# A two-layer graph network kernel: folded softmax sums, packed score columns and a finer hand-written order

## The chip, the cores and the metric

The kernel runs on one core of a Trainium2 chip. The metric is the device time of one execution in microseconds (us); less is better. The engines are named as in the profile: PE (matrix products; PEld is its weight load), DVE (vector), ACT (scalar and activation functions), POOL (general) and SP, which here only issues transfers (DMA).

## The reference

128 graphs of 128 nodes with 256 features pass a transformer-like layer with masked values and then a two-fold graph attention, each with a feed-forward part (FFN) and two norms.

```python
# layer 0, 8 heads of 32
scores = einsum('bhid,bhjd->bhij', q, k) / sqrt(dh)
attn = softmax(scores, axis=-1)
for r in range(4):
    out = out + einsum('bhij,bhjd->bhid', attn * (adj == r), v_r)
x = ln(src + out @ Wo + bo)
x = ln(x + gelu(x @ W1 + b1) @ W2 + b2)
# layer 1, twice: e = leaky_relu(Wh1 + Wh2^T), masked by adj > 0
att = softmax(where(adj > 0, e, NEG), axis=1)
h = att @ Wh
x = ln(x + h); x = ln(x + relu(x @ w1 + b1) @ w2 + b2)
```

adj holds only 0 and 1, so two of the four value products suffice; the kernel checks that at run time.

## The kernel before

One straight program handles 32 groups of 4 graphs (512 tokens, G = 4, P = 128, T = 512). All is float32, and each product of the program is two records in the profile. Of each group, `projected` computes q, k and v, `attention` the first layer's attention, `ffn` (called as `first_ffn` and `second_ffn`) the two feed-forward parts, `layer1` the graph attention, `norm`, `sent` and `turned` the norms and the turning of the tokens (planes of 16 bits, a transposing DMA into pT, and copies into yT). Projections and FFNs use seven block products for eight; ffn keeps one chain of them in the PSUM bank called seeded and the others in fa and fe.

The order of the work is written out by hand. FRONT, STEADY and TAIL are strings of tokens. `a:1` means: take the next step of the attention of the group one behind the base group; `*n` repeats it. Each function is a generator, and what stands between two `yield`s is one step. The names: `q` projected, `a` attention, `f` and `k` first and second FFN, `l` layer1, `n0` to `n3` norm, `t0` to `t2` turned, `bo` prepared, `in` and `rest` loads, `out` store; `gelu` and `exp` touch a function table. FRONT starts the pipeline, STEADY runs once for each of 29 base groups (a "turn"), TAIL ends it. Every engine executes its own instructions strictly in the order in which the tokens issue them; an instruction that waits holds all that come behind it on its engine, and on SP all transfers behind it. Tiles with one buffer are taken again only when their last reader has finished.

Steps that the change touches, with line numbers of the profile:

- `scores` (751, 759): products ps of q and k for a pair of graphs, 32 rows of the array each, and four Exp activations into e, a tile of 4 x 2 x 2 x 128 columns: four heads s, two graphs u of the pair, two halves c of the heads, 128 target nodes i. The 128 partitions are the source nodes.
- `masked` (769): pm = e times the adjacency, four products on DVE.
- `sums` (787, 801): pav, the value products with e and pm, and pden, the sum over all source nodes by a product with ones, four of 512 columns in 32-column tiles of the array. Then on DVE the transposes, the range checks and the reciprocal (813 to 819), and oT = pav times it (825). A pair 0 puts pden into bank fe, a pair 1 into one of the two banks s.
- `spread` (875 to 886): one score column of each of four graphs is laid along a row on all partitions, either directly (products with the identity, groups 0, 31 and in part 30) or by a transpose on PE (880), a DVE copy (882) and two transfers through DRAM (885, 886).
- `edges` (894 to 911): Identity with bias, leaky ReLU, Exp, the mask with its sums, the division.
- `prepared` (589, 593): the output bias is added to x, and a DVE instruction sums adj (adj - 1) to check it.
- `variances` (352, 354), `root` (369, 370), `affine` (381), `store` (958): the norms and the output. The variances of norm 3 stay in c_out for a check at the end.
- In `ffn` (454 to 571) a product, its evacuation and often several DVE instructions are one step.

The attention's product with ones, before:

```python
def plain():
    for s in range(HC):
        nc.tensor.matmul(
            pden[s * DH : (s + 1) * DH], k.ones, e[:, s], start=True, stop=True
        )
```

Of the kernel before, what the change touches and what calls it, by code (L numbers as in the profile page):

```python
# [31 lines left out]
class Weights:  # L32


    def __init__(self, tc, const, a):
        self.tc, self.nc, self.const, self.a = tc, tc.nc, const, a
        self.queue = tc.nc.scalar

# [3 lines left out]
    def w(self, name, t=None):  # L42
        w = self.a[name]
        if t is None:
            t = self.tile([P, w.shape[0] // P, w.shape[1]], "w_" + name)
        self.nc.sync.dma_start(t, w.rearrange("(c p) n -> p c n", p=P))
        return t

    def col(self, name, t=None):
# [3 lines left out]
        with self.nc.allow_non_contiguous_dma(reason="a bias vector as columns"):  # L53
            self.queue.dma_start(t, v.rearrange("(c p) -> p c", p=P))
        return t

    def row(self, name, first=None, t=None):
# [5 lines left out]
        if t is None:  # L63
            t = self.tile([P, n], "r_" + name)
        self.queue.dma_start(
            t, bass.AP(tensor=v.tensor, offset=v.offset, ap=[[0, P], [1, n]])
# [3 lines left out]
    def row_sum(self, n1, n2, t=None):  # L70
        r1, r2 = self.row(n1), self.row(n2, t=t)
        self.nc.gpsimd.tensor_add(r1, r1, r2)
        return r1

    def constants(self):
# [3 lines left out]
        self.ones = self.tile([P, P // 4], "ones")  # L79
        nc.vector.memset(self.ones, 1.0)  # L80
        self.eps = self.tile([P, 1], "eps")
        nc.vector.memset(self.eps, EPS)
        self.lo = self.tile([P, 1], "lo")
        nc.vector.memset(self.lo, LO)
        self.none = self.tile([1, 1], "none")
        self.mhalf = self.tile([P, G], "mhalf")
        nc.vector.memset(self.mhalf, -0.5)

# [14 lines left out]
q:0*6 a:0*3 q:0 a:0*2 b1 bo:0 a:0*2 q:1*2 a:0 q:0 q:1 gw q:1 w1 a:0 a:1 a:0 a:1 a:0*2 wqk a:1 a:0  # L103
q:1*2 n0:0 q:1 n0:0*2 a:1 n0:0 a:1*2 n0:0 a:1*3 gelu t0:0 q:1 w2 a:1 t0:0*2 f:0 a:1 in:2
output_bias f:0 a:1 f:0*2 bo:1 f:0*2 a:1 f:0 q:2 a:1 q:2 gw q:2 f:0*2 q:2 f:0 gw n0:1 f:0 q:2
f:0*2 n0:1 gw q:2 f:0*3 n0:1 f:0 n0:1 f:0*3 q:2 f:0*2 t0:1 n0:1 t0:1 n1:0 f:1 n1:0 t0:1 n1:0*2 c1
f:1*2 n1:0 q:2 f:1 q:2 t1:0 f:1 q:2 f:1 t1:0 f:1 q:2*2 u2 l:0 f:1 l:0 f:1 q:2 l:0 wv l:0*2 f:1
q:2 u1 q:2 a:2 l:0 a:2 f:1 l:0 f:1*2 l:0 f:1*2 l:0 q:2 l:0 a:2 q:2 l:0*4 q:2*2 f:1*2 q:2 l:0 exp
q:2 n2:0 q:2*4 n2:0*3 f:1 q:2 n2:0 f:1 q:2*3 t2:0 f:1 t2:0 f:1
"""  # L110
STEADY = """
f:0 a:1*2 k:-1 a:1 n1:0 t2:-1 a:1 in:2 n1:0 a:1 k:-1*2 a:1 k:-1 n1:0 k:-1*3 n1:0 a:1 n1:0 t1:0
k:-1*2 a:1 bo:1 l:0 k:-1 a:1 k:-1 a:1 t1:0 k:-1*2 a:1 k:-1 l:0 k:-1 n0:1 l:0 k:-1 n0:1*4 k:-1 q:2
k:-1 q:2 l:0 k:-1 t0:1 l:0 t0:1 q:2 k:-1*2 q:2 l:0 t0:1 f:1*4 l:0*2 q:2 k:-1 f:1 n3:-1 f:1*2 l:0
f:1 q:2*2 l:0 f:1 n3:-1*2 f:1 q:2*2 gelu f:1*3 q:2*2 out:-1 f:1 q:2 l:0 q:2 l:0 q:2*2 l:0 f:1 a:2
l:0 f:1 q:2 a:2 rest:2 q:2*2 a:2 q:2 l:0 n2:0 q:2 f:1 q:2*3 n2:0*2 f:1 q:2*2 n2:0 q:2 f:1 q:2*3
n2:0 t2:0 exp f:1 t2:0 f:1
"""
TAIL = """
f:0 a:1 n1:0 a:1 t2:-1 in:2 k:-1*2 a:1*2 k:-1 n1:0*2 k:-1 a:1*2 k:-1*2 a:1 n1:0*2 a:1 k:-1 t1:0  # L120
k:-1 l:0 a:1 k:-1*2 bo:1 k:-1 a:1*2 t1:0 l:0*2 k:-1 n0:1 k:-1 n0:1 k:-1 n0:1 k:-1 l:0 n0:1 k:-1*2
n0:1 l:0*2 t0:1 l:0 k:-1*3 l:0*2 t0:1 k:-1 l:0*2 t0:1 l:0 k:-1 f:1*2 l:0 f:1*2 gelu l:0 f:1*2 l:0
f:1 n2:0 f:1 n3:-1 f:1*5 n2:0*2 f:1*4 n2:0*2 exp f:1 t2:0*2 f:1*4 n1:1 t2:0 n1:1 k:0*3 n1:1*2 k:0
n1:1 k:0*2 t1:1*2 k:0 q:2 l:1 k:0 l:1 n3:-1 l:1*4 k:0 l:1 k:0*2 l:1*3 n3:-1 l:1*3 k:0*2 l:1 k:0*2
l:1 n2:1 k:0 n2:1 k:0 out:-1 n2:1*2 k:0 n2:1 k:0 t2:1 k:0 t2:1 k:0 t2:1 k:0 k:1*2 n3:0 k:1*12
n3:0 k:1*3 n3:0 checks k:1 out:0 k:1*2 z:1*2 k:1*2 z:1
# [11 lines left out]
def fast_pass(ctx, tc, a, out):  # L138
# [275 lines left out]
    def turned(S, i):  # L414
        n = f"{i}_{S['g']}"
        S["xT", i + 1] = yT = w2p.tile([P, NCH, T], F32, tag="yT", name="yT_" + n)
        for p in range(G // 2):
# [6 lines left out]
            if p == 0:  # L424
                yield
# [971 lines left out]
```

## Time and profile before

| | us |
|---|---|
| median of 3 runs (2649.4 to 2652.24) | 2651.66 |
| the profiled execution | 2648.62 |
| its span, first to last instruction | 2646.8 |

The mean granted PE clock was 0.997. In the profile's span PE was busy 2617.9 us, DVE 2229.0, ACT 1672.5, POOL 133.3, and the DMA engines moved 136.43 MB. Of the chain that ended last, the product with ones (pden) makes 2%, ps 3%, pav and pw 4% each; the two FFNs' products (po, ph and seeded) make 58%.

Lines of the groups view read: line, engine, operation, output from input, shapes, count, busy time and mean ns of one, and idle time ahead of it with what ended it. Instructions of one engine overlap at their ends, so busy time divided by count is less than the mean. Lines of the chain read: start, length until the next link, engine, tile, line, count.

### The profile page before, as it was taken

What the parts mean: (1) busy time and instruction counts of PE and PEld (TensorE: products, weight loads), DVE (VectorE), ACT (ScalarE), POOL (GpSimd) and SP (SyncE); (2) the same over time, 40 slices, a digit from 0 to 9 for tenths busy, and PEclk for the clock granted to TensorE, in tenths of its full rate; (3) what the DMA queues carried; (4) which work ended last, traced back from release to release, by engine and by line L of the source; (5) the groups of instructions that cost most, each with busy time, mean ns of one, the idle gap of its engine ahead of it and who ended that gap; (6) DMA issues with size and microseconds to landing.
All of it is one profiled execution on the core that took longest, in us unless ns stands there. A gap on an engine that the chain in (4) does not pass through costs nothing.

```text
span 2646.8 us, 53404 instructions
## 1 busy us (share of the span) xinstructions
PE 2617.9 (99%) x20917; PEld 2308.3 (87%) x20917; DVE 2229.0 (84%) x5804; ACT 1672.5 (63%) x3519; POOL 133.3 (5%) x137
## 2 busy tenths in 40 slices
PE   9999999999999999999999999999999999999997
PEld 6888898888988888988889988889888889888886
DVE  5788888888888889888888888888888888888876
ACT  3666667666666566676666675666666666756663
POOL 0000000000000000000000000000000000000000
PEclk9999999999999999999999999999999999999999
DMA  6111222121212122222212121222122121212211
GB/s 176 34 37 49 60 53 45 37 61 49 53 45 58 40 51 59 53 45 40 57 49 55 47 57 37 53 57 53 45 46 52 49 57 47 55 37 56 46 29 34
DMA packets 271899, 136.43 MB, mean 52 GB/s; under 512 B 210092, under 2 KB 250392, under 8 KB 271640
## 3 DMA queue, kind: packets, MB, share of 16 engines
q1 hardware_dynamic: 270536, 132.55, 21.3%
q8 instruction: 166, 2.72, 0.4%
q14 instruction: 93, 0.76, 0.1%
q10 hardware_dynamic: 1104, 0.40, 0.1%
HBM read 65.68 MB, written 16.90 MB: 31 GB/s over the span
## 4 chain that ended last, share of the span: by engine, by line
PE 95%; DVE 2%; ACT 1%; DMA 1%; issue 0%; POOL 0%; POOLq 0%; ACTq 0%; DVEq 0%
PE po L463 17%; PE ph L454 16%; PE seeded L454 13%; PE seeded L463 12%; PE pw L922 4%; PE pav L801 4%; PE pwo L838 4%; PE pvqa L681 4%; PE pqqa L681 4%; PE pvqb L681 3%; PE pqqb L681 3%; PE ps L751 3%; PE py L935 2%; PE pg L948 2%; PE pden L787 2%; DMA pT<-planes 1%
## 5 line engine op out<-in xcount | busy, mean ns | idle before, releaser
L395 ACT COPY planes<-x 128x512 uint16<-128x512 uint16 x384 | 218.5, 617 | 290.2 <-DVE x L381 288.0
L421 ACT COPY yT<-pT 128x512 uint16<-128x512 uint16 x384 | 266.8, 765 | 94.3 <-DMA pT<-planes 93.8
L370 POOL TENSOR_TENSOR rs<-rs,mhalf 128x4 f32<-128x4 f32 x129 | 131.2, 1017 | 2459.9 <-DVE rs L369 2413.3
L454 PE MATMUL seeded<-yS,w_L_gnn_w_ff 128*128 128x256 f32 x768 | 206.0, 391 | 2.0 <-DVE hT L510 0.8
L759 ACT ACTIVATE e<-ps 128x512 f32<-128x512 f32 x256 | 134.9, 597 | 107.2 <-PE ps L751 107.2
L454 PE MATMUL seeded<-yS,w_L_gnn_W 128*128 128x256 f32 x768 | 200.6, 384 | 1.3 <-ACT seeded L527 0.7
L352 DVE BATCH_NORM_STATS2 st<-x 128x6 f32<-128x256 f32 x512 | 192.4, 418 | 7.7
L454 PE MATMUL ph<-yT,w_L_gnn_w_ff 128*128 128x256 f32 x768 | 195.3, 383 | 0.0
L454 PE MATMUL ph<-yT,w_L_gnn_W 128*128 128x256 f32 x768 | 192.4, 379 | 0.0
L454 PEld LDWEIGHTS seeded<-yS,w_L_gnn_w_ff 128*128 128x128 f32 x768 | 137.5, 189 | 61.5 <-DVE h L523 23.5
L463 PEld LDWEIGHTS po<-w_L_gnn_W,hT 128*128 128x128 f32 x1536 | 186.2, 192 | 5.0 <-ACT hT L478 0.3
L463 PE MATMUL po<-w_L_gnn_w_ff,hT 128*128 128x128 f32 x1536 | 187.1, 275 | 0.0
L463 PE MATMUL po<-w_L_gnn_W,hT 128*128 128x128 f32 x1536 | 187.1, 275 | 0.0
L463 PEld LDWEIGHTS po<-w_L_gnn_w_ff,hT 128*128 128x128 f32 x1536 | 181.7, 192 | 1.8
L454 PEld LDWEIGHTS seeded<-yS,w_L_gnn_W 128*128 128x128 f32 x768 | 142.2, 190 | 29.0 <-ACT seeded L492 7.0
L454 PEld LDWEIGHTS ph<-yT,w_L_gnn_w_ff 128*128 128x128 f32 x768 | 143.1, 190 | 22.7 <-ACT hT L478 1.0
L454 PEld LDWEIGHTS ph<-yT,w_L_gnn_W 128*128 128x128 f32 x768 | 145.5, 190 | 19.9 <-issue 0.2
L478 ACT ACTIVATE hT<-hT,c_L_gnn_b_ff 128x256 f32<-128x256 f32 x256 | 109.2, 497 | 83.8 <-DVE hT L510 83.8
L769 DVE TENSOR_TENSOR pm<-e,adj 128x512 f32<-128x512 f32 x256 | 159.0, 682 | 1.7 <-ACT e L759 1.7
L510 DVE TENSOR_TENSOR hT<-seeded,p 128x512 f32<-128x512 f32 x128 | 87.6, 684 | 62.3 <-ACT hT L478 31.0
L478 ACT ACTIVATE hT<-hT,c_L_gnn_b 128x256 f32<-128x256 f32 x256 | 109.1, 497 | 31.4 <-DVE hT L510 29.6
L922 PE MATMUL pw<-wu,yT 128*128 128x260 f32 x512 | 124.6, 385 | 2.5 <-ACT yT L421 2.1
(195 smaller groups left out, 6085.2 us busy)
## 6 DMA issues: line engine op xcount, KB each, us to landing
xT<-in_xT_dram SPq DMA_DIRECT2D x32, 512.0 KB, 3.9
x<-in_x_dram SPq DMA_DIRECT2D x32, 512.0 KB, 6.5
out_dram<-x SPq DMA_DIRECT2D x31, 512.0 KB
spread<-hbm SPq DMA_DIRECT2D x59, 256.0 KB, 3.1
adj<-in_adjT_dram SPq DMA_DIRECT2D x32, 256.0 KB, 3.7
pT<-planes SPq DMA_TRANSPOSE x192, 3.1
w_L_gnn_W<-in_L_gnn_W_dram SPq DMA_DIRECT2D x8, 256.0 KB, 8.7
w_L_gnn_w_ff<-in_L_gnn_w_ff_dram SPq DMA_DIRECT2D x8, 256.0 KB, 5.7
```

The source lines that it names most:

```text
L352: nc.vector.bn_stats(st[:, b % 2, :], S["x"][:, b, :])
L370: nc.gpsimd.tensor_tensor(rs[:, bs], rs[:, bs], k.mhalf[:, bs], op=ALU.pow)
L395: nc.scalar.copy(planes[:, :, b], words)
L421: nc.scalar.copy(o.rearrange("p (b t h) -> p h b t", b=2, h=2), pT[:, :, :, c, :])
L454: nc.tensor.matmul(bank[:, s * TH : (s + 1) * TH], wa[:, form, 0, f * P : (f + 1) * P], m, start=start and s == 0, stop=True, skip_group_c ...
L463: nc.tensor.matmul(bank[:, s * P : (s + 1) * P], m[:, f, s * P : (s + 1) * P], wb_[:, form, f, :], start=start and s + f == 0, stop=True, ...
L478: nc.scalar.activation(o[:, s], o[:, s] if src is None else src[:, s * TH : (s + 1) * TH], func, bias=ba[:, f : f + 1],)
L681: nc.tensor.matmul(bank[:, s * TH : (s + 1) * TH], *ops, start=start and s == 0, stop=True, skip_group_check=True,)
L759: nc.scalar.activation(e[:, s], pss[s], AF.Exp, scale=SCALE)
L769: nc.vector.tensor_mul(pm[:, s], S["e", p][:, s], S["ad"][:, pair(p), None, :].to_broadcast([P, 2, NCH, P]),)
L801: nc.tensor.matmul(pav[s * DH : (s + 1) * DH, u, c, :], v[:, d0 : d0 + DH], m[:, s, u, c, :], start=(r == 0), stop=(r == 1),)
L922: nc.tensor.matmul(pw[:, :NU], yT[:, c, b * P : (b + 1) * P], wu[:, c, :], start=(c == 0), stop=(c == NCH - 1),)
```

## The change

Four things are changed.

The product with ones gets its operand folded. A tile es holds, for each head, the exponentials of the upper half of the source nodes of one graph added to those of the lower half; the two graphs of a pair take the two halves of the partitions. So 256 columns are left of 512, and `split`, two blocks of ones, keeps the graphs apart. To bring the halves together, four transfers for each pair move half of e to the other 64 partitions, ACT copies the other half into a part of pm that isn't yet in use, and DVE adds. `folded` is a generator of its own, with the token `d`.

The score column that goes through DRAM is no longer transposed on PE: `own`, four values on each partition, is written as 16-byte rows, and the row that comes back is read with a stride of four. Group 0 takes this path too.

The check of adj moves from DVE to ACT (Square of adj - 0.5, with the sum), and c_out becomes one tile of 4 x 2 for all groups, to which `root` adds zero times the variances.

The order is new and finer. Products, evacuations and single DVE instructions are steps of their own, the seeded chain of an FFN is a generator of its own (`fc`, `kc`), loads of weights are steps (`Lqk` and so on), and FRONT, STEADY and TAIL are written anew. small2 gets two buffers; x21 and x22 take the tags p16 and p7; the planes of norm 0 share a tag with es.

```diff
+        self.split = self.tile([P, P // 4], "split")
+        nc.vector.memset(self.split, 0.0)
+        for h in range(2):
+            nc.vector.memset(
+                self.split[h * P // 2 : (h + 1) * P // 2, h * P // 8 : (h + 1) * P // 8], 1.0
+            )
...
 STEADY = """
+fc:0 q:1 d:1 q:1 fc:0 f:0 d:1 n2:-1*2 t2:-1*2 q:1 f:0 a:1 fc:0 a:1 f:0 fc:0 t2:-1 a:1*2 t2:-1
+k:-1 t2:-1 a:1 fc:0 a:1 kc:-1 t2:-1 d:1 a:1 k:-1 a:1 k:-1 a:1 kc:-1 d:1 rest:1 n1:0 kc:-1 a:1
+n1:0 d:1*2 a:1*2 k:-1*2 a:1 k:-1 a:1 k:-1 kc:-1 d:1 kc:-1 d:1 a:1 d:1 k:-1 in:2 d:1 k:-1*2 n1:0
+a:1 kc:-1*2 a:1 n1:0*2 kc:-1*2 a:1 bo:1 kc:-1 a:1 kc:-1 a:1 k:-1 kc:-1 a:1*2 n1:0*2 a:1 kc:-1
+t1:0*2 a:1 kc:-1 t1:0 a:1 k:-1 l:0 kc:-1 bo:1 a:1 l:0*2 kc:-1 t1:0 kc:-1 a:1 l:0 a:1 n0:1 k:-1*3
+l:0*2 q:2 n0:1 l:0 kc:-1 q:2 k:-1 l:0 kc:-1 bo:1 k:-1 l:0 n0:1 kc:-1 k:-1 kc:-1*3 q:2*2 n0:1*3
+kc:-1*2 n0:1 l:0*3 k:-1 t0:1 k:-1 t0:1 k:-1 kc:-1 k:-1 kc:-1*3 k:-1 kc:-1 l:0 k:-1 t0:1 f:1 t0:1
+l:0 kc:-1 q:2 t0:1 fc:1 l:0 t0:1 f:1 l:0*2 f:1*3 l:0*2 fc:1*2 q:2 l:0 f:1 kc:-1 q:2 l:0 q:2 f:1
+l:0*3 fc:1 l:0 rest:2 f:1 l:0 fc:1 l:0 n3:-1 f:1 l:0*2 fc:1*3 f:1 fc:1 n3:-1 fc:1 n3:-1 fc:1*2
+q:2 f:1 fc:1 q:2*2 fc:1 q:2 f:1*2 fc:1 f:1 fc:1 q:2 f:1 fc:1 q:2 f:1 fc:1 gelu q:2*2 fc:1 q:2
+l:0*3 fc:1 f:1 l:0 q:2 a:2 l:0 f:1 fc:1 l:0 fc:1 a:2 l:0 q:2 l:0*2 a:2 l:0 exp l:0 a:2*2 q:2 l:0
+a:2 f:1 q:2 d:2 a:2 l:0 q:2 l:0*2 fc:1 d:2 q:2 l:0 d:2 fc:1 d:2 q:2*2 d:2 a:2 l:0 fc:1 n2:0 q:2
+n2:0*2 q:2 out:-1 n2:0 q:2 fc:1 f:1 n2:0 q:2 d:2 f:1 fc:1
 """
...
         scr = w1p.tile([P, G, P], F32, tag="gs", name=f"scr_{g}")
-        nc.vector.scalar_tensor_tensor(
-            flat(scr), flat(ad), 1.0, flat(ad),
-            op0=ALU.subtract, op1=ALU.mult, accum_out=c_adj[:, g : g + 1],
+        nc.scalar.activation(
+            flat(scr), flat(ad), AF.Square, bias=k.less, accum_out=c_adj[:, g : g + 1]
         )
...
+        if i == 3:
+            nc.vector.scalar_tensor_tensor(
+                c_out[:, bs], S["mv", i][:, bs], 0.0, c_out[:, bs], op0=ALU.mult, op1=ALU.add
+            )
...
+        def others():
+            begun(0)
+            yield
+            for r in range(RN):
+                pe = ps_1.tile([P, T], F32, tag="fe", name=f"ph7_{n}_{r}")
+                product(pe, T3, S["yS", i][:, 2], r, True)
+                yield
+                B["7", r] = w1p.tile([P, T], F32, tag="p7", name=f"p7_{n}_{r}")
+                nc.scalar.copy(B["7", r], pe)
+                yield
+                product(B["a", r], B21, a12, r)
+                yield
+                activated(B["a", r], r, 0, 0)
+                yield
+                product(pe, T4, a22, r)
+                yield
+                nc.vector.tensor_add(hidden(0, 1, r), halves(pe), halves(B["16", r]))
+                yield
+                activated(None, r, 0, 1)
+                yield
+                if r + 1 < RN:
+                    begun(r + 1)
+                    yield
...
+        def chain():
+            nc.scalar.copy(seeded, B["a", 0])
+            yield
+            s1, s2, _, s4 = (S["yS", i][:, m] for m in range(4))
+            for r in range(RN):
+                rs = slice(2 * r, 2 * r + 2)
+                product(seeded, T2, s2, r)
+                yield
+                B["16", r] = w1p.tile([P, T], F32, tag="p16", name=f"p16_{n}_{r}")
+                nc.scalar.copy(B["16", r], seeded)
+                yield
+                product(seeded, T1, s1, r)
+                yield
+                nc.vector.tensor_add(hidden(1, 1, r), halves(seeded), halves(B["7", r]))
+                yield
+                activated(None, r, 1, 1)
+                yield
+                product(seeded, B22, s4, r)
+                yield
+                activated(seeded, r, 1, 0)
+                yield
+                nc.vector.tensor_sub(h3[:, rs], hidden(0, 0, r), hidden(0, 1, r))
+                yield
+                nc.vector.tensor_add(hidden(0, 1, r), hidden(0, 1, r), hidden(1, 1, r))
+                yield
+                nc.vector.tensor_sub(h2[:, rs], hidden(1, 1, r), h3[:, rs])
+                yield
...
+    def folded(S):
+        n = str(S["g"])
+        for p in range(G // 2):
+            e = S["e", p]
+            S["es", p] = es = w1p.tile([P, HC, NCH * P], F32, tag="es", name=f"es_{n}_{p}")
+            for h in range(2):
+                hs = slice(2 * h, 2 * h + 2)
+                for lo in range(2):
+                    to, fr = (slice(x * P // 2, (x + 1) * P // 2) for x in (lo, 1 - lo))
+                    nc.sync.dma_start(
+                        es[to, hs], e[fr, hs, lo].rearrange("p s c i -> p s (c i)")
+                    )
+                yield
+            for h in range(2):
+                hs = slice(2 * h, 2 * h + 2)
+                ea = S["pm", p][:, 2 + h].rearrange("p u c i -> p u (c i)")
+                for lo in range(2):
+                    own = slice(lo * P // 2, (lo + 1) * P // 2)
+                    nc.scalar.copy(ea[own], e[own, hs, lo].rearrange("p s c i -> p s (c i)"))
+                    yield
+                nc.vector.tensor_add(es[:, hs], es[:, hs], ea)
+                yield
 
...
-        pden = pool.tile([P, 2, NCH, P], F32, tag=tag, name="pden_" + n)
+        pden = pool.tile([P, T], F32, tag=tag, name="pden_" + n)[:, : NCH * P]
         pav = ps_1.tile([P, 2, NCH, P], F32, tag="av", name="pav_" + n)
 
         def plain():
             for s in range(HC):
                 nc.tensor.matmul(
-                    pden[s * DH : (s + 1) * DH], k.ones, e[:, s], start=True, stop=True
-                )
-        late = S["g"] > 1
-        if not late:
-            plain()
+                    pden[s * DH : (s + 1) * DH], k.split, S["es", p][:, s], start=True, stop=True
+                )
+        assert {(1, 0, p), (1, 1, p)} <= S["have"]
         for u in range(2):
             v = S["v"][:, 2 * p + u]
             for c in range(NCH):
@@ -803,35 +927,38 @@
                             v[:, d0 : d0 + DH], m[:, s, u, c, :],
                             start=(r == 0), stop=(r == 1),
                         )
-        if late:
-            plain()
-        g, oT = S["g"], S["oT"]
         yield
+        plain()
+        g = S["g"]
+        yield 1
         rd = w1p.tile([P, 2, NCH, P], F32, tag="rd", name="rd_" + n)
         flat_rd = rd.rearrange("p u c i -> p (u c i)")
-        nc.vector.transpose(flat_rd, pden.rearrange("p u c i -> p (u c i)"))
-        each = flat_rd[:, ::DH]
+        nc.vector.transpose(flat_rd[:, : NCH * P], pden)
+        each = flat_rd[:, : NCH * P : DH // 2]
         nc.vector.tensor_reduce(c_att[:, 0, g, p : p + 1], each, AX.X, ALU.min)
         nc.vector.tensor_reduce(c_att[:, 1, g, p : p + 1], each, AX.X, ALU.add)
-        rc = small.tile([P, T // DH], F32, tag="rc", name="rc_" + n)
-        nc.vector.reciprocal(rc, each)
+        yield
+        rc = small2.tile([P, T // DH], F32, tag="rc", name="rc_" + n)
+        nc.vector.reciprocal(rc.rearrange("p (u k) -> p k u", u=2), each.rearrange("p (k u) -> p k u", u=2))
         nc.vector.transpose(
             flat_rd.rearrange("p (k r) -> p k r", r=DH), rc[:, :, None].to_broadcast([P, T // DH, DH])
         )
-        yield
+        yield 1
+        if p == 0:
+            S["oT"] = w1p.tile([P, NCH, T], F32, tag="oT", name=f"oT_{g}")
         for u in range(2):
             bs = slice((2 * p + u) * P, (2 * p + u + 1) * P)
-            nc.vector.tensor_mul(oT[:, :, bs], pav[:, u], rd[:, u])
-        yield
+            nc.vector.tensor_mul(S["oT"][:, :, bs], pav[:, u], rd[:, u])
+            yield u or None
 
...
     def spread(columns, n, direct):
 
 
-        pr = ps_s.tile([P, T], F32, tag="s", name="pr_" + n)
         if direct:
+            pr = ps_s.tile([P, T], F32, tag="s", name="pr_" + n)
             for b in range(G):
                 nc.tensor.matmul(
                     pr[:, b * P : (b + 1) * P], columns[:, b : b + 1].to_broadcast([P, P]), k.ident,
                     start=True, stop=True,
                 )
             return pr.rearrange("p (b i) -> p b i", b=G)
-        nc.tensor.transpose(pr[:G, :P], columns, k.ident)
-        line = small2.tile([G, P], F32, tag="line", name="line_" + n)
-        nc.vector.tensor_copy(line, pr[:G, :P])
         t = w1p.tile([P, G, P], F32, tag="spread", name="spread_" + n)
-        hbm = dram.tile([G, P], F32, tag="hbm", name="hbm_" + n)
-        nc.sync.dma_start(hbm, line)
+        own = small2.tile([P, G], F32, tag="own", name="own_" + n)
+        nc.vector.tensor_copy(own, columns)
+        hbm = dram.tile([P, G], F32, tag="hbm", name="hbm_" + n)
+        nc.sync.dma_start(hbm, own)
         nc.sync.dma_start(t, hbm.partition_broadcast(P))
-        return t
+        return t.rearrange("p b i -> p (b i)").rearrange("p (i b) -> p b i", b=G)
 
```

## The prediction

> **What bounds the kernel now.** I read the page first: busy shares and the chain that ended last.
>
> ```profile
> PE 2617.9 (99%) x20917; PEld 2308.3 (87%) x20917; DVE 2229.0 (84%) x5804; ACT 1672.5 (63%) x3519; POOL 133.3 (5%) x137
> ...
> PE 95%; DVE 2%; ACT 1%; DMA 1%; issue 0%; POOL 0%; POOLq 0%; ACTq 0%; DVEq 0%
> ```
>
> A busy PE of 99% alone proves little, because the ends of matmuls are modelled; that 95% of the chain is PE, waiting for nobody, does. Next I took stretches. One steady turn (a group of 512 tokens) repeats every 80.58 us; this is turn 1265 to 1345.58, and beside it a piece of the tail (columns: elapsed, then busy and count of PE, PEld, DVE, ACT, POOL).
>
> ```profile
> 1265.00:1345.58 80.58, 80.58 (x653) 71.70 (x652) 69.25 (x181) 52.26 (x111) 4.07 (x4) 1.00 0.20 50
> ```
> ```profile
> 2560.00:2600.00 40.00, 33.48 (x199) 28.02 (x199) 27.97 (x81) 26.17 (x57) 1.04 (x1) 1.00 0.15 34
> ```
>
> In the turn PE never idles and DVE is at 86%; the tail leaves PE idle. Then the chain of waits inside that turn (start, length, engine, tile), which gives what each product really costs in a stream:
>
> ```profile
> 1283.41 1.88 PE pav L801 x64
> 1285.30 0.86 PE pden L787 x8
> 1286.15 1.10 PE ps L751 x32
> 1287.26 1.92 PE ph L454 x8
> 1289.18 0.93 PE seeded L454 x4
> 1290.11 0.86 PE ph L454 x4
> 1290.97 1.11 PE seeded L454 x4
> ...
> 1295.69 0.86 PE pden L787 x8
> 1296.55 1.06 PE seeded L454 x4
> ...
> 1311.54 0.11 PE pr L880
> ```
>
> The product with ones, pden, is 0.86 us, twice a turn. The transpose of the score column, pr, is 0.11, twice a turn. A four-record FFN product is 0.86 undisturbed, an eight-record one 1.73 (pwo at 1301.96), so 0.07, 0.25 and 0.20 are lost on seeded and 0.19 on ph after ps. Adding all pieces at their undisturbed price gives 79.60; about 1.0 us a turn is loss.
>
> **What the Trainium skill says.** (1) "TensorE: Matmul & The Clock Gate", Part 3 (packing small matmuls): matmuls with 32 output columns, in different column groups, run at the same time. The trace agrees: eight pden records of 512 columns take 0.86, as long as four of 256 on the whole array, and eight pav records of 128 columns 0.22; the cost follows the columns streamed. (2) "TensorEngine Tiling", Key Properties: changing the tiling mode drains the engine. The trace agrees: 0.19 and 0.20 lost where an FFN product follows ps or pden. (3) "DMA: Bandwidth & Descriptors", Specifications: pieces under 512 B are read, modified and written. No trace of before has 16-byte rows; its own have 512 B. (4) "Advanced Engine Details and Errata", SBUF Cachelines: an access pattern that takes a new 16-byte line at each element is slower. Nothing before reads an SBUF tile so.
>
> **The change on PE.** pden streams 256 columns where it streamed 512: 64 times 0.43 gone, 27.5 us. The pr transposes go: 59 times 0.11, 6.5; group 0 now takes the DRAM path too, so its two direct spreads of 0.9 each (pr at 121.73 and 135.16 in the chain) go, 1.8. PE work removed: 35.8 us, of which 1.08 in each of 29 steady turns. I wrote out the new STEADY step by step: every step of a turn occurs once, pav and pden still stand next to each other on PE, followed by ps for the first pair and by pwo for the second. So no mode change is added, and pricing the PE steps gives 78.52 a turn. The split of product and evacuation into separate tokens adds no PE instruction.
>
> **What is added elsewhere, a turn.** Rows for it (mean ns after the busy time):
>
> ```profile
> L769 DVE TENSOR_TENSOR pm<-e,adj 128x512 f32<-128x512 f32 x256 | 159.0, 682 | 1.7 <-ACT e L759 1.7
> L813 DVE STREAM_TRANSPOSE rd<-pden 128x512 f32<-128x512 f32 x64 | 45.3, 708 | 0.6 <-PE pden L787 0.6
> L882 DVE COPY line<-pr 4x128 f32<-4x128 f32 x59 | 16.3, 276 | 25.1 <-PE pr L880 25.1
> L593 DVE SCALAR_TENSOR_TENSOR scr<-adj 128x512 f32<-128x512 int32 x32 | 21.9, 683 | 0.5 <-issue 0.5
> L500 ACT COPY p<-ph 128x512 f32<-128x512 f32 x128 | 76.0, 594 | 15.1 <-PE ph L454 15.0
> ```
>
> DVE: four fold additions of 128x512 at 0.62 (159.0/256), +2.5; the adjacency check (0.68 and 0.08 for the accumulator) leaves for ACT, -0.8; two half transposes, -0.6 to -0.7; two copies of 0.28 become about 0.16, -0.2; the c_out step +0.17. Net +1: 70.3 of about 79.5, 88%. ACT: eight half-partition copies at 0.59 (row L500; no row has 64 partitions, so the bound is 0.3 to 0.6 and I take the upper end), +4.7, and the Square, about +0.6: 57.6, 72%. Neither becomes the bound by its sum. A table load for Square would add up to 2.6 a turn (1.28 twice), still cover.
>
> **Where the cover is thin.** Sums over a turn hide order, so I took the stretch in which the second pair's fold stands, from the end of the first FFN's last T4 product (po) to where pav of that pair reads its last masked tile. PE between: 1.79 + 1.88 + 0.43 + 1.10 + nine products of 0.864 + 0.3 = 13.3. DVE in the same tokens, by the spacing of back-to-back instructions in the timeline, as here (0.60):
>
> ```profile
> 1342.01 0.68 DVE L525 TENSOR_TENSOR h<-hT,h 128x512 f32<-128x512 f32 x1
> 1342.61 0.68 DVE L727 TENSOR_TENSOR qT<-pqqb,pq 128x512 f32<-128x512 f32 x1
> ```
>
> Nine of 0.60 (5 masked, 2 fold, 2 hidden sums), eight of 0.34 (2 FFN, 4 yS, 2 oT), two statistics pairs of 1.0, one affine pair 1.58, and denominators with their small ones 1.55: 13.25. That is no slack; the same sum for before is 10.2 on PE against 9.2 on DVE, and there pm ended at 1373.56 and pav began at 1374.39, so the method is right to some 0.2. On ACT, from ps to the last fold copy: 6.5 of 6.9. I expect 0.2 to 0.4 us of new waiting at the second FFN's first B22 product on seeded, or at pav of the second pair,, and take it equal to what the finer steps recover of the 0.4 that PE now waits for seeded copies (0.07 and 0.25 above, 0.07 again in the second FFN). The bounds of this pair of effects are -0.4 and +1.0 a turn, -12 and +29 in all.
>
> **Transfers.** SP gets eight transfers of 128 KB a turn (64 partitions to the other 64), in order with pT, x, xT, adj, hbm, spread and out. Landing times now:
>
> ```profile
> x<-in_x_dram SPq DMA_DIRECT2D x32, 512.0 KB, 6.5
> ...
> spread<-hbm SPq DMA_DIRECT2D x59, 256.0 KB, 3.1
> ...
> pT<-planes SPq DMA_TRANSPOSE x192, 3.1
> ```
>
> For 128 KB I take 2.7: the skill's "SBUF — State Buffer" (Door 1, and the setup-cost knee) gives 196 GB/s for 64 partitions and about 2 us fixed; an estimate, between 2.5 and the 6.5 of x. The tight one is the second transfer of the second pair: e of its last head is ready 2.6 after ps, its addition is due at 6.9, so it has 4.3 us. adj, x and xT of the next turns come behind it on SP, so only out and pT stand ahead. SP waits for e in front of them, but their consumers are turns away or 7 us later (pT of n2). The hbm step writes 16-byte rows: 0 to +2 us before the spread returns; the copy own stands some 3.5 us of PE ahead of its first consumer on ACT, and behind that consumer PE has five 1.79 products, so I cost it at nothing. SP, which now waits 0.9 for hbm each time, holds pT of n0 behind it up to 2 us longer, five products ahead of its reader. The strided read of target costs ACT 0 to 0.4 on each of eight 0.39 instructions, also inside ACT's slack.
>
> **Front and tail.** Before, the first steady turn starts at 154.1 and the tail takes 2493.9 to 2646.8. Pricing the PE steps of both orders gives about 138.8 (119.5 of groups 0 to 2, warm-ups 5.3, the weight set-up 12.2, direct spreads 1.8) and 125.4, so about 15 and 27.5 us are loss. The new FRONT also orders the loads; products start at 6.65 after four warm-ups, as before, if the first loads are no later. Splitting lets second_ffn's chain and others fill the layer1 chain of the last group (PE 33.48 of 40 us above). I take 4 us, bounds -5 and +15 gained.
>
> **Sum.** -35.8 - 4 + 0 = -39.8. The profiled execution took 2648.6 (span 2646.8 plus 1.8), so 2608.8; the runs shown have a median of 2651.66, 3.0 higher, so 2611.8, taken as **2611**.
>
> **Rivals.** (A) The forecast: PE stays the bound, the product is halved, waits balance. 2600 to 2622; 60%.
> (B) The order pays as well: the 0.4 a turn goes without new waits (-12), and front and tail give 10: 2593; 12%. For: PE's losses are small waits that finer steps can fill. Against: the zero slack above.
> (C) Fold waits eat half: 0.7 a turn at the same two places, 20 us: 2631; 17%. For: the DVE sum, 13.25 of 13.3.
> (D) Slower: the second pair's transfer lands late and stops DVE in order at its addition; behind it stand pm1.3, then pav, and PE. It costs from 4.3 us of landing on and decides from 5.7, where 1.4 a turn eats the 39.8. With x's 6.5: 2.2 times 29 = 64, 2675. For: a 512 KB row does take 6.5, and SP issues in order. Against: pT of the same 128 KB lands in 3.1, and the DMA share is 0.20; 7%.
> (E) The halved stream doesn't halve the time (weight loads or drain bound pden): 0.2 gained instead of 0.43, 64 times 0.23 less: 2626; 4%. Against: pav's 128-column records do scale.
>
> **Numbers.** Range 2592 to 2638: it leaves out D, the low end of B and the high end of C. What tells a change from none here is about 0.2%, 5.3 us. Faster 0.89 (A, B, E, nearly all of C), within 0.03 (the end of C), slower 0.08 (D and a little of C).
>
> **What would show it.** Right: pden 0.43 in the chain, no pr, a steady turn of 79.2 to 79.9, PE still above 94% of the chain, es landing under 4 us. Wrong: a turn over 80.6; DVE waiting for DMA es; PE waiting for pm or for hT of the hidden sum before that B22 product; pden far from pav; a table load at Square; or a front that reaches its first steady turn later than 154 less the work moved out of it.

## The result

The changed kernel takes 2645.97 us in the median of 20 runs (2643.69 to 2652.65), the kernel before 2650.78 beside it; ratio 0.9985, 95% interval [0.9978, 0.9992]. It is faster by 4.8 us where 39.8 were forecast, below the 0.2% that was set as the border of what can be told from no change.

The page of the changed kernel: span, busy shares, chain that ended last, and the groups and transfers of the fold.

```profile
span 2648.2 us, 54505 instructions
PE 2603.5 (98%) x20842; PEld 2309.2 (87%) x20842; DVE 2246.1 (85%) x5907; ACT 1859.7 (70%) x3839; POOL 132.8 (5%) x137
...
PE 74%; DVE 14%; ACT 8%; issue 2%; DMA 2%; SPq 0%; POOL 0%; DVEq 0%; ACTq 0%; POOLq 0%
...
L871 DVE TENSOR_TENSOR pm<-e,adj 128x512 f32<-128x512 f32 x256 | 172.2, 683 | 2.9 <-ACT e L862 0.7
L896 ACT COPY pm<-e 64x512 f32<-64x512 f32 x256 | 157.8, 616 | 1.6
...
es<-e SPq DMA_DIRECT2D x256, 128.0 KB, 2.4
...
spread<-hbm SPq DMA_DIRECT2D x61, 256.0 KB, 3.9
```

PE's share hardly moves, 99% to 98%; its share of the chain falls from 95% to 74%. In the turn shown next the chain leaves PE at 876.36 for 25 us of DVE and ACT work and comes back at 901.52 (start, length, what):

```profile
875.48 0.88 PE pvqa L785 x4
876.36 0.02 issue
876.38 0.59 ACT pv L802
...
900.63 0.85 ACT hT L545 x2
901.48 0.04 issue
901.52 1.99 PE ph L521 x8
```

Two stretches answer to those shown before (elapsed, then busy and count of PE, PEld, DVE, ACT, POOL, then clock, DMA share, GB/s).

```profile
824.38:904.39 80.01, 79.77 (x652) 71.56 (x656) 69.71 (x185) 58.01 (x122) 4.03 (x4) 1.00 0.27 64
2560.00:2600.00 40.00, 35.64 (x217) 29.90 (x216) 29.72 (x83) 27.44 (x61) 2.36 (x2) 1.00 0.14 27
```

An undisturbed turn is 80.01 where 79.2 to 79.9 were forecast; the tail stretch is fuller. From the starts of the score products ps I took three parts of each profiled execution: up to the first ps of group 3, the 28 turns from there, and the rest.

```
                 to group 3   28 turns: mean (undisturbed)   rest    span
before             214.97        80.68  (80.57)             172.8   2646.8
changed            229.16        80.39  (80.01)             168.2   2648.2
```

So the steady turns gained 8.2 us where some 30 were forecast (28 times 1.08), the rest gained 4.6, and the front lost 14.2. (The profiled execution of the changed kernel, 2649.95, is some 4 us above its median; one trace does not show in which part that lies, so the 14.2 may be more than a median run loses.)

The new wait of a steady turn, on PE's timeline: start, length, line, product, and in brackets the idle time before it with what ended it.

```profile
894.14 0.61 PE L913 MATMUL pden<-es,split 128*32 128x256 f32 x8
894.68 1.17 PE L855 MATMUL ps<-qT,kT 32*128 32x128 f32 x32
895.79 1.13 PE L521 MATMUL ph<-yT,w_L_gnn_w_ff 128*128 128x256 f32 x4
...
900.27 1.03 PE L521 MATMUL seeded<-yS,w_L_gnn_w_ff 128*128 128x256 f32 x4
901.52 1.13 PE L521 MATMUL ph<-yT,w_L_gnn_w_ff 128*128 128x256 f32 x4 [0.22 <-ACT hT L545]
```

pden takes 0.54 from its start at 894.14 to that of ps at 894.68. With 512 columns, in the kernel before, it is 0.97 to the next product:

```profile
1295.51 1.04 PE L787 MATMUL pden<-e,ones 128*32 128x512 f32 x8
1296.48 1.13 PE L454 MATMUL seeded<-yS,w_L_gnn_w_ff 128*128 128x256 f32 x4
```

The product at 900.27 normally lets the next one start 0.86 later; here it is 1.25, as ph waits for a bank that the activation hT frees. ACT at the same time:

```profile
898.87 0.63 ACT L625 COPY p<-seeded 128x512 f32<-128x512 f32 x1
899.34 1.26 ACT L896 COPY pm<-e 64x512 f32<-64x512 f32 x2
900.63 0.84 ACT L545 ACTIVATE hT<-ph,c_L_gnn_b_ff 128x256 f32<-128x256 f32 x2
901.36 1.24 ACT L896 COPY pm<-e 64x512 f32<-64x512 f32 x2
```

Two half copies of the fold, together 1.26, stand right ahead of that activation.

The front, in the chain of waits (start, length, engine, what) and in stretches of 4 us:

```profile
63.21 2.05 ACT e L862 x4
65.26 0.66 ACT yT L489
65.92 0.34 SPq L887
66.26 0.06 issue
66.31 0.60 SPq L887
66.91 0.04 issue
66.95 0.59 SPq L51
67.55 0.04 issue
67.59 4.72 DMA temp<-in_L_gnn_b_ff_dram
72.31 0.02 issue
72.33 0.04 ACTq L545
72.37 0.03 issue
72.40 1.28 ACT L545
73.68 0.01 issue
73.70 0.84 ACT hT L545 x2
```
```profile
72.00:76.00 4.00, 0.09 (x1) 0.10 (x2) 1.17 (x3) 2.65 (x5) 0.72 (x1) 0.95 1.09 287
76.00:80.00 4.00, 3.22 (x54) 2.79 (x58) 2.34 (x4) 1.59 (x4) 0.00 (x0) 0.50 0.09 21
```

SP issues the es transfers (L887) once e is there; the load of a bias row into temp stands behind them, and the first hT, which takes over temp's buffer, waits for it. v, masked scores and pav stand behind hT in order. PE does 0.09 us of work in the 4 us from 72, and in the next stretch its granted clock is 0.50. The Trainium skill, "TensorE: Matmul & The Clock Gate", Part 1, has PE's clock halved after an idle window of about 3.4 us until it has been busy as long again; the trace agrees, with 4.4 us of idle time here and a grant of 0.5 in pieces of 3.4 and 6.8 us. The first 160 us, in the kernel before and then in the changed one; the mean granted clock falls from 0.97 to 0.91:

```profile
0.00:160.00 160.00, 153.09 (x1226) 122.04 (x1227) 112.08 (x288) 78.58 (x158) 7.42 (x13) 0.97 0.36 94
0.00:160.00 160.00, 144.13 (x1024) 113.29 (x1024) 100.99 (x262) 84.85 (x167) 5.73 (x11) 0.91 0.41 104
```

### The profile page after: what moved, and what is told of

Read it like the earlier page. It is cut to its first block, busy times and chain, and to the rows that moved or that the text cites. A ratio compares the mean times of both kernels' runs of the same rounds, so it can differ in the third digit from the quotient of the medians.

```text
span 2648.2 us, 54505 instructions
## 1 busy us (share of the span) xinstructions
PE 2603.5 (98%) x20842; PEld 2309.2 (87%) x20842; DVE 2246.1 (85%) x5907; ACT 1859.7 (70%) x3839; POOL 132.8 (5%) x137
## 4 chain that ended last, share of the span: by engine, by line
PE 74%; DVE 14%; ACT 8%; issue 2%; DMA 2%; SPq 0%; POOL 0%; DVEq 0%; ACTq 0%; POOLq 0%
PE po L530 15%; PE ph L521 12%; PE seeded L521 10%; PE seeded L530 9%; PE pw L1042 4%; PE pwo L965 4%; PE pqqa L785 4%; PE pqqb L785 3%; PE pav L925 3%; DVE x L441 2%; ACT pm L896 2%; PE py L1055 2%; DVE st L407 2%; PE pvqa L785 2%; ACT e L862 2%
## 5 line engine op out<-in xcount | busy, mean ns | idle before, releaser
L521 PE MATMUL seeded<-yS,w_L_gnn_w_ff 128*128 128x256 f32 x768 | 199.9, 383 | 2.9 <-DVE yS L501 1.8
L871 DVE TENSOR_TENSOR pm<-e,adj 128x512 f32<-128x512 f32 x256 | 172.2, 683 | 2.9 <-ACT e L862 0.7
L896 ACT COPY pm<-e 64x512 f32<-64x512 f32 x256 | 157.8, 616 | 1.6
L545 ACT ACTIVATE hT<-hT,c_L_gnn_b_ff 128x256 f32<-128x256 f32 x256 | 115.7, 501 | 26.1 <-DVE hT L629 22.9
L1042 PE MATMUL pw<-wu,yT 128*128 128x260 f32 x512 | 130.6, 387 | 2.7 <-ACT yT L489 2.6
```

The lines of the kernel that those rows point to most:

```text
L521: nc.tensor.matmul(bank[:, s * TH : (s + 1) * TH], wa[:, form, 0, f * P : (f + 1) * P], m, start=start and s == 0, stop=True, skip_group_c ...
L545: nc.scalar.activation(o[:, s], o[:, s] if src is None else src[:, s * TH : (s + 1) * TH], func, bias=ba[:, f : f + 1],)
L871: nc.vector.tensor_mul(pm[:, s], S["e", p][:, s], S["ad"][:, pair(p), None, :].to_broadcast([P, 2, NCH, P]),)
L896: nc.scalar.copy(ea[own], e[own, hs, lo].rearrange("p s c i -> p s (c i)"))
L1042: nc.tensor.matmul(pw[:, :NU], yT[:, c, b * P : (b + 1) * P], wu[:, c, :], start=(c == 0), stop=(c == NCH - 1),)
```

## The experiments

Times are medians; each ratio is to the kernel before, run on the same chip (2648.74 to 2650.58 there). "Turn" is the mean of the 28 turns, then the undisturbed one.

**The fold alone undone (nofold).**

```diff
-    pden[s * DH : (s + 1) * DH], k.split, S["es", p][:, s], start=True, stop=True
+    pden[s * DH : (s + 1) * DH], k.ones, e[:, s], start=True, stop=True
```
(in effect, for all groups; with the whole transposition of pden as before, and nothing issued in the steps d)

> The changed kernel with the fold alone undone: the product with ones streams all 512 columns of e again, no es transfer, no half copy, no fold addition; order, spread and loads as changed. Theory G (the fold saves its 27.5 us on PE and gives most of it back by what it puts on SP, ACT and DVE): PE work +27.5, waits back -10 (the wait of PE for hT in the second FFN, 0.35 in each of 29 turns), irregular waits -6, front -10: 2640 to 2652, about the changed kernel's 2646. Theory O (the fold is nearly free, the new order loses the gain): 2646 + 27.5 less at most 5, 2668 to 2674, slower than both kernels.

2639.46, ratio 0.9959 [0.9946, 0.9972]: 6.5 us below the changed kernel. Turn 80.42 (80.41), ps of group 3 at 215.24, rest 168.1. Its page:

```profile
PE 2605.9 (99%) x20842; PEld 2304.5 (87%) x20842; DVE 2200.5 (84%) x5779; ACT 1719.6 (65%) x3583; POOL 133.0 (5%) x137
...
PE 97%; DVE 1%; ACT 1%; issue 0%; SPq 0%; DMA 0%; POOL 0%; DVEq 0%; POOLq 0%; ACTq 0%
```

The order is not what loses: without the fold PE is 97% of the chain, and every turn is alike to 0.1 us. It follows that in a steady turn the fold takes 2 times 0.43 off PE and gives 0.83 back, and that in the profiled executions it costs some 14 us ahead of group 3. The front without the fold is no shorter than before, 215.24 against 214.97; what the order gains besides lies in the turns (80.42 against 80.68) and in the rest (168.1 against 172.8).

**The fold undone in the front alone (nofold_front): groups 0 and 1.**

```diff
+        if S["g"] < 2:
+            for _ in range(16):
+                yield
+            return
```
(and whole streams of e in these two groups)

> The fold undone in groups 0 and 1 alone, which are the front; steady part as changed. Theory G for the front (es transfers on SP stand ahead of the loads, DVE stops in order for them, PE falls idle and its clock is then halved for some us): the four full streams cost 1.7 more, the idle stretches at 20 to 24 and 72 to 77 us and the half clock behind them go, 6 to 10: 2636 to 2642, first pav of the second group's steady turn some 5 to 8 us before 169. Theory O (the order of the front loses, whatever the fold does): 2647 to 2648.

2637.82, ratio 0.9951 [0.9938, 0.9964], 8.2 less than the changed kernel although PE has 1.7 more to do. ps of group 3 at 217.76 instead of 229.16; turn 80.40 (80.01), as in the changed kernel. The front's loss is the fold's: 11.4 us in these two traces and 8.2 by the medians, each beside 1.7 of work added. In the steady part the fold is worth nothing.

**A possible cause in the front (temp_early): the bias rows loaded earlier.** The middle of one of the lines changed:

```diff
-d:1 Lgat n0:0 a:1 Lh1 n0:0 t0:0*2 w1
+d:1 Lgat n0:0 a:1 Lh1*3 n0:0 t0:0*2 w1
```
(and the two later Lh1 dropped)

> The row of biases that is loaded into temp, the buffer that the first hT takes over, and its addition on POOL are issued some 11 us earlier in FRONT, ahead of the es transfers of the second group; nothing else. Theory G for the front: the stretch 71.5 to 77.3 us in which PE is idle for 5 us goes, and with it the half clock that follows for 6.8 us (3.4 us of work): 7 to 9 less, 2637 to 2640. Rival (masked scores and es additions of the second group are as late by themselves): at most 2 less, 2644 to 2646.

In the profiled execution the idle stretch of PE at pav shrinks (longest wait 2.5 instead of 4.4) and ps of group 3 comes at 220.94, 8.2 earlier. But the median of 22 runs is 2646.82, from 2638.48 to 2651.69, and the profiled execution, 2639.76, is the third fastest of them. The runs differ with their mean granted clock: ten at 0.993 have a median of 2649.08, four at 0.996 or 0.997 took 2638.48 to 2640.48. Inconclusive: that this wait stood there is seen, that its end alone brings time is not.

**Two moves against the two short waits (steady_order).** Parts of the lines changed:

```diff
-n1:0 d:1*2 a:1*2 k:-1*2 a:1 k:-1 a:1 k:-1 kc:-1 d:1 kc:-1 d:1 a:1
+n1:0 a:1*2 k:-1*2 d:1*2 a:1 k:-1 a:1 k:-1 kc:-1*2 d:1*2 a:1
-exp l:0 a:2*2 q:2 l:0 a:2 f:1 q:2 d:2
+exp l:0 a:2*2 q:2 a:2 f:1 q:2 l:0 d:2
```

> Two moves in STEADY and nothing else: the two half copies of the second pair's first fold on ACT go behind the activation whose bank the next ph product waits for, and the product pg0 goes behind the second v product. Theory W (in a steady turn PE loses 0.35 at ph for ACT's queue and 0.26 at pg for the copies out of its bank, nothing else new): undisturbed turn 79.4 instead of 80.0, 29 times 0.6 = 17.7 less, 2628 to 2632. Rival D (DVE, in order, is as late at pav of the second pair, so the wait only moves there): turn 79.8 to 80.1, 2640 to 2646.

2655.64, ratio 1.0017 [1.0011, 1.0024]: slower than both kernels. Turn 80.52 (80.39). The wait at ph is gone and another stands in its place, in PE's waits over the steady turns (line, released by, us in total, times, longest):

```profile
PE pav L925 <- DVE pm L871: 10.6, 27, 0.5
```

The later copy makes the fold addition later, the addition frees the tile of pm that the next masked score writes, and pav of the second pair reads that. Product by product against an undisturbed turn of the changed kernel, the end of the wait at ph gives 0.5, pav and what follows it take 0.75, and the move of the product pg0 (layer 1) takes 0.1 instead of giving 0.26. The turns explain 3.7 us; where the rest of the 9.7 between the medians lies is not shown. I expected 17.7; the moves only showed that copy, addition and masked score are one chain.

**Parts of the fold left out:** no_copy drops the first line below, no_add the second, no_transfer the third, no_copy_add the first two. Where one operand is missing, the addition adds the other to itself.

```diff
-    nc.scalar.copy(ea[own], e[own, hs, lo].rearrange("p s c i -> p s (c i)"))
-    nc.vector.tensor_add(es[:, hs], es[:, hs], ea)
-    nc.sync.dma_start(es[to, hs], e[fr, hs, lo].rearrange("p s c i -> p s (c i)"))
```

> Leaves out the eight half-partition copies a turn on ACT (the addition adds es to itself, so the sums of the product with ones are not the reference's); transfers and additions stay. A turn is now 80.39 in the mean, 80.43 with the fold undone, and 79.56 would be 80.43 less twice 0.43. Theory A (ACT's queue takes the gain: copies ahead of hT): turn 79.6 to 79.7, 20 to 23 us less, 2623 to 2626. Theory D (the additions on DVE, in order among the masked scores): 80.0 to 80.3, 3 to 10 less. Theory X (transfers of es, and the pT transfers beside them, come late): 80.2 to 80.4.

> Leaves out the four fold additions a turn on DVE (the product with ones reads what was transferred alone, so its sums are not the reference's); transfers and copies stay. Theory A: ph still waits for hT behind the copies, turn 79.9 to 80.1. Theory D: turn 79.6 to 79.7, and the front loses its stops at the additions too, 2622 to 2630. Theory X: the irregular half of the loss stays, 80.0.

> Leaves out the eight es transfers a turn on SP's queue (the addition adds the copied half to itself, so the sums are not the reference's); copies and additions stay. Theory X: the irregular part goes, turn 79.9 to 80.0, and the front, in which loads no longer stand behind es on SP, comes 8 to 12 earlier: 2622 to 2630. Theories A and D: turn 80.3 to 80.4; the front gains the same 8 to 12: 2634 to 2638.

> Leaves out the eight half copies and the four fold additions (the product with ones reads what was transferred, so its sums are not the reference's); the transfers stay. Theory C (copy on ACT and addition on DVE hold all that the fold gives back in a steady turn: 0.48 at ph, 0.25 at pav with the copies gone, the rest late transposes): undisturbed turn 79.55 to 79.60, mean under 79.7, 20 us under the 2646 of the changed kernel or more, 2620 to 2628. Rival (something else of the fold, its transfers or the new product itself, holds a part): undisturbed turn above 79.7.

```
              median   ratio [95%]               turn: mean (undisturbed)
no_copy       2636.06  0.9943 [0.9926, 0.9959]    79.97  (79.79)
no_add        2644.41  0.9980 [0.9969, 0.9991]    80.22  (80.00)
no_transfer   2640.54  0.9956 [0.9940, 0.9973]    80.33  (80.01)
no_copy_add   2619.79  0.9890 [0.9874, 0.9907]    79.63  (79.56)
```

No single part held it, as each theory had it. Without copies ph no longer waits, and pav then waits for a masked score behind the additions, 0.23 a turn. Without additions ph waits as before. Without transfers a turn is unchanged (80.33 against 80.39), but in the one trace ps of group 3 comes at 223.40, 5.8 of the front's 13.9 us earlier. Without both copies and additions the undisturbed turn is 79.56, which is 80.41 less twice 0.43 to within 0.02; the chain of that run:

```profile
PE 96%; DVE 1%; ACT 1%; DMA 1%; issue 0%; SPq 0%; POOL 0%; ACTq 0%; DVEq 0%; POOLq 0%
```

So copies on ACT and additions on DVE hold all that the fold gives back in a turn. The irregular part (turns of 80.2 to 81.4) has the same source; the kernel before has five turns of 81.0 to 81.4 too, nofold none. Transposed loads pT (of the normed tokens; the copies yT and layer 1's product pw follow them) land after 3.1 us in the median and up to 6.3 (6.1 without the fold). Those of norm 1 are issued 9.39 us after ps of the second pair without the fold or without the copies, 10.70 with them, as the planes are copied on ACT behind the half copies; pw comes 15.5 after ps in both. What PE's weight loads waited for there, in the changed kernel and then without the fold:

```profile
PEld ph L521 <- ACT hT L545: 17.4, 28, 0.6
...
PEld pw L1042 <- ACT yT L489: 8.6, 17, 1.1
```
```profile
PEld pw L1053 <- ACT yT L489: 0.2, 1, 0.2
```

**The fold on POOL (pool_fold): no copy on ACT, no addition on DVE.**

```diff
-    nc.scalar.copy(ea[own], e[own, hs, lo].rearrange("p s c i -> p s (c i)"))
-    nc.vector.tensor_add(es[:, hs], es[:, hs], ea)
+    half = e[own, hs, lo].rearrange("p s c i -> p s (c i)")
+    nc.gpsimd.tensor_add(es[own, hs], es[own, hs], half)
```

> The fold computed in full, but on POOL: es plus the other half of e at 64 partitions, eight additions a turn of some 1.4 us (estimated from 0.72 for 128x256 on POOL), no copy on ACT and no addition on DVE; transfers stay. Theories A and D together: turn 79.6 to 79.9, 14 to 22 less, 2624 to 2632. Rival (POOL is late: two additions after the last transfer take 2.8 and pden of the second pair waits for them, and the powers of the norms queue behind them): turn above 80.4, 2650 or more.

2714.46, ratio 1.0240 [1.0223, 1.0257]; turn 82.58, some 61 us more over the 28 turns. The rival's wait is there: POOL's additions take 1.51, and pden waits for them 23 times, 14.5 in all. That is a quarter of it; no theory had that beside them DVE is slower as well:

```profile
L897 POOL TENSOR_TENSOR es<-es,e 64x512 f32<-64x512 f32 x256 | 385.7, 1507 | 650.2 <-DMA es<-e 612.8 <-ACT p L625 14.6 <-ACT qT L720 7.3
...
L871 DVE TENSOR_TENSOR pm<-e,adj 128x512 f32<-128x512 f32 x256 | 211.1, 845 | 0.0
```

The same masked score took 683 in the changed kernel. The Trainium skill, "SBUF — State Buffer", "SBUF: two separate sides", says that GpSimd and a DVE instruction with two inputs in SBUF take one pair of ports in turn, the whole instruction long; the masked score is such an instruction, and 162 ns more in the mean agree. Products on PE then wait for DVE, as seeded does for a hidden sum (13.7 in all).

**The fold off the path, twice (late_fold, late_fold2).** Copies behind the activation, additions behind the last masked score, copies into other tiles than pm; whole streams in groups 0, 1 and 31. The lines of the tile alone, without its name:

```diff
-                ea = S["pm", p][:, 2 + h].rearrange("p u c i -> p u (c i)")
+                ea = w1p.tile([P, 2, NCH * P], F32, tag=("spread", "gs")[h])
```

> The fold kept for groups 2 to 30 and taken off the path: the half copies on ACT write two idle tiles (those of the graph part, spread and gs) instead of the last two tiles of pm, go behind the activation that ph waits for, and the additions on DVE go behind the last masked score, ahead of the product with ones alone; groups 0, 1 and 31 stream e whole. Theory C (copy, addition and masked score are one chain in pm's tiles, and its two ends are the two waits of PE): undisturbed turn 79.56, mean 79.6 to 79.8, front as with the fold off there: 2636 to 2640 less 18 to 24, 2614 to 2622. Rival L (ACT and DVE are short of time as such, the waits only move): turn 80.2 to 80.5, 2634 to 2642.

2890.40, ratio 1.0906 [1.0891, 1.0921], and it tells nothing of the question: spread and gs also carry the planes of norms 1 and 2, so that these wait for the additions (ACT's waits):

```profile
ACT planes L461 <- DVE es L906: 300.7, 50, 11.7
```

late_fold2 takes parts of h3 and h2 of the FFN that has done with them or has not come to them yet (set against late_fold):

```diff
-                ea = w1p.tile([P, 2, NCH * P], F32, tag=("spread", "gs")[h])
+                if p == 0:
+                    ea = lent[1, S["g"] - 1][1][:, 2 * h : 2 * h + 2]
+                else:
+                    ea = lent[3, S["g"] - 2][1 - h][:, 2:4]
```

> The fold kept in full for groups 2 to 30, whole streams of e for groups 0, 1 and 31. The half copies write parts of h2 and h3 that are idle then, not the last tiles of pm; they stand behind the activation that ph waits for; both additions stand behind the last masked score. (The run before of this kind lent the copies the tiles of the norms' planes, which were not idle.) Theory C: undisturbed turn 79.55 to 79.70, mean 79.6 to 80.0 as the copies still stand ahead of the planes of norm 1: 2637.8 less 14 to 24, 2614 to 2624. Rival L (ACT or DVE is short of time whatever the order): undisturbed turn 80.0 or more, 2632 to 2642.

2640.57, ratio 0.9964 [0.9950, 0.9978]; turn 80.42 (80.27). The 0.48 at the first ph is gone; 0.5 comes back at pwo (the attention's output product), which waits for an addition of the residual on DVE, and 0.2 at two ph products. My theory that only the place of copy and addition counts is not borne out: in this order too the stretch from the last T4 product to pwo has no time to spare on DVE for two more additions. Other orders were not tried.

**Two other parts: the score columns (before_spread) and the front's clock (nofold_wide).**

```diff
-        nc.tensor.transpose(pr[:G, :P], columns, k.ident)
-        nc.vector.tensor_copy(line, pr[:G, :P])
+        nc.vector.tensor_copy(own, columns)
```
(in the kernel before; transfers and read of the spread as changed)

> The kernel before, with the new score columns alone: no transpose pr on PE, a copy of the strided column on DVE, 16-byte rows to DRAM, a strided read on ACT. The prediction's price: 59 transposes of 0.11, 6.5 less, and one mode of tiles the same: turn 80.36, 2644 to 2645. Rival (the strided read on ACT and the later landing, 3.9 against 3.1, come onto the path): turn 80.5 to 80.8, 2649 to 2654.

2643.77 beside 2649.84, ratio 0.9977 [0.9967, 0.9987]: 6.1 less; turn 80.48 (80.42). The packed columns alone bring at least about as much as the whole change; the two intervals overlap.

```diff
-                    col[:, c : c + 1], start=(c == 0), stop=(c == NCH - 1),
+                    col[:, c : c + 1].to_broadcast([P, 64]), start=(c == 0), stop=(c == NCH - 1),
```
(in nofold, for the 32 matmuls of each pbias, whose sums are subtracted from a bias; one of each 64 equal columns is then read)

> The changed kernel without the fold (2639.5), and the 32 matmuls of each pbias, which stream one column each for 3.5 us, stream 64 equal columns of which one is read. Theory K (the clock is halved after a stretch in which PE streams few columns or none, so the stretch of 1.7 lost behind pbias goes): no half-clock piece in the first 160 us, or not within 10 us of a pbias, 2637 to 2639, pbias itself no longer than 3.6. Rival (the halving has another cause): a piece of 3.4 or 6.8 us at half clock stays within 10 us after the second pbias; time within 1 of 2639.5.

2637.32, ratio 0.9952 [0.9938, 0.9965]. The same stretch behind the second pbias (100.2 to 103.9) in nofold and in nofold_wide; the column before the last two is the granted clock:

```profile
104.00:108.00 4.00, 4.00 (x13) 3.29 (x13) 2.89 (x7) 2.35 (x6) 0.00 (x0) 0.61 0.34 66
```
```profile
104.00:108.00 4.00, 4.00 (x20) 3.49 (x19) 2.58 (x6) 3.65 (x8) 0.00 (x0) 1.00 0.34 66
```

The reduced clock behind pbias is gone, at the same length of pbias; one such piece of 3.4 us came at 121 us instead, after PE had waited 3.0 for kT. Two pbias without a piece prove little by themselves: in the fourteen other traces, which stream one column, a piece begins during 22 of the 28 pbias or within 5 us behind them, and in the other six (the first of nofold and both of no_copy_add among them) none does. Beside this, the mean granted clock is 0.998 in all five runs here, and 0.996 to 0.998 in nofold's. The time is 2.1 lower than nofold's, which the intervals do not part. With nofold_front it is the fastest version here that computes everything.

## Why the prediction was wrong

The measured medians divide the change so: packed columns -6.1 (before_spread), order, finer steps and the small moves of work -4.8 (nofold's ratio against before_spread's, 0.18% of 2650; the two intervals leave some 4 us of play), fold +6.5 (changed against nofold). As each share is the step from one kernel to the next, that they sum to -4.4 beside the -4.8 measured is no further proof.

- **pr, 6.5:** measured 6.1. Right. **Front and tail 4, direct spreads 1.8:** together 5.8 against 4.8 without the fold. The size is right, the place was luck: nofold's front gained nothing (215.24 against 214.97) although its direct spreads had gone, its tail gained 4.7, and its turns lost a little less to short waits. The front of the order with the fold in it was another thing, see below.
- **pden 0.43, 27.5 in all:** right as work on PE: 0.97 to 0.54 and 0.55 per product, and 79.56 a turn once nothing waits; 80.58 less 1.08 is 79.50. Rival E falls.
- **Durations added:** nearly right. Half copies 0.62 (0.59 taken, at the upper end of its bound), Square 0.72 and 0.20 for its accumulator (0.6), strided read 0.52 instead of 0.39 on each of eight (0 to 0.4 allowed). That nothing before reads an SBUF tile with a wide step was wrong: the range checks read rd at every 32nd column, though no dense reading stood beside it. The spread landed after 3.9 instead of 3.1 (0 to 2 more allowed), es after 2.4 (2.7 taken). No table load was added, 65 in both. Rival D falls: without transfers the turn stays.
- **Waits in the steady turns, taken as 0 between -0.4 and +1.0 a turn: this is the step that failed.** It was 0.83, 23 us over 28 turns: about 0.45 in every turn, the rest in the irregular ones. The prediction's own count found 13.25 us of DVE in 13.3 of PE, called this "no slack", and then set it equal to what finer steps might recover. With no slack, what the count misses becomes a wait. And the count on ACT ended with the last half copy; the activation behind it, whose bank ph takes over, was left out, and that is where PE waited first. Of the two places named, pav of the second pair showed in full only when the copies were away or later; the B22 product was not among PE's waits. Rival C had the kind of wait and nearly its size (0.7 a turn), not the place, and should have been the forecast.
- **Front and tail -4, bounds -5 to +15 gained: failed too.** The front lost 14.2 in the trace, of which the fold is nearly all (nofold: 215.24); the rest behind the turns gained 4.6. The prediction had no term for the fold in the front. SP was followed in the steady turn, where only pT and out stood behind es, not in FRONT, where the weights' loads share that queue; and nobody asked what a PE idle for 4 us gets as its clock afterwards. How the loss divides between transfers, additions and clock stays open: 5.8 of it went with the transfers, in one trace, and 0.06 less of granted clock over 160 us is at most 9.6 us of full clock (an estimate from the two rows above).
- **The tests named:** no pr, pden 0.43, es under 4, no load of a table held; turn 79.2 to 79.9, PE above 94% of the chain and a front no later than 154 less the work moved out failed. Together they said where the gain went before an experiment ran: the undisturbed turn 0.5 too long, and 14 us in the front.

What stays open: why the mean granted clock, with which the runs of temp_early go, differs from run to run, and how much of the front's 14 us each half-clock piece holds. The runs leave also open whether a fold at other places of a turn, where DVE has slack, would pay.

## What to carry to other kernels

Work taken off the busiest engine is worth only what its neighbours can still hand over in time: count the stretch between the consumer's reads, with everything behind the new instructions on each queue, and where the count says zero slack, forecast waits; here they took back 0.83 of the 0.86 a turn. Leave a new step out by its parts and in pairs: a turn without one part was 0.4 or 0.2 shorter, without both 0.8, as the second wait stands behind the first. In a front where loads and transfers share a queue, a step that waits for data holds every load behind it, as es held temp here.

## What was not expected of the hardware

- A copy of 64 partitions and 512 columns on ACT takes 616 ns in the mean, no less than one of 128 partitions does (p from PSUM, 589; planes, of 16-bit values, 615).
- PE's granted clock was 0.5 for pieces of 3.4 or 6.8 us. They began during or close behind idle time of PE (4.4 us at 72 us in the changed kernel), and also during or within 5 us behind most rows of 32 matmuls of one streamed column with no idle time among them (22 of 28 rows). Streaming 64 columns instead cost 273 against 247 ns a record, no more time in the row, and no piece followed in the one trace of it (two rows).
- An ACT instruction that reads 128x128 with a step of 16 bytes took 517 to 520 ns where the dense one took 389 to 394.
